# A conditioned convolution and feed-forward kernel: two more weight sums on GpSimd, one more convolution in short form, another order at both ends

## The chip, the cores and the metric

The kernel runs on one core of one Trainium2 chip. All data are fp32. The metric is the device time of one execution in microseconds (us). Engines are named as the profile names them: PE is TensorE's matmul, PEld its weight load, DVE is VectorE, ACT is ScalarE, POOL is GpSimd, SP is SyncE (used here to issue DMA transfers).

## The reference, cut to what matters

The input x has 128 samples of 64 channels by 1024 positions. Two layers are added to it, each a small mixing step followed by a matrix over the 1024 positions.

```python
def _L0_cond_ref(x, embedding, W0, b0, W1, b1, W2, b2, weight, bias_k):
    h = jax.nn.gelu(embedding @ W0 + b0, approximate=False)
    h = jax.nn.gelu(h @ W1 + b1, approximate=False)
    att = jax.nn.softmax((h @ W2 + b2) / T, axis=-1)
    agg_w = jnp.einsum('bk,koi->boi', att, weight[..., 0])   # 8 experts, 64x64, one matrix per sample
    agg_b = att @ bias_k
    return jnp.einsum('boi,bih->boh', agg_w, x) + agg_b[:, :, None]

def _L0_ffn_ref(x, A, B, bias):                              # rank 128
    return jnp.einsum('bsd,od->bso', x, A @ B.T) + bias

def _L1_cond_ref(x, c, weight, c_weight, bias):              # 9 taps, 4 groups of 16 channels
    out = lax.conv_general_dilated(x, weight, ..., padding=[(4, 4)], feature_group_count=4)
    return out + (c @ c_weight.T)[:, :, None] + bias[None, :, None]

def _L1_ffn_ref(x, W_up, gate_w, expert_bias, lora_A, lora_B):
    x_flat = x.reshape(-1, 1024)
    one_hot = top1(x_flat @ gate_w.T + expert_bias)          # 4 experts
    base_out = x @ W_up.T                                    # 1024 x 1024
    delta = lora_B[e] @ (lora_A[e] @ x_flat), e = one_hot    # rank 8
    return base_out + delta

x = x + _L0_ffn_ref(_L0_cond_ref(x, cond_128, ...), ...)
x = x + _L1_ffn_ref(_L1_cond_ref(x, cond_128, ..., fside_S_0), ...)
```

## The kernel before

**Tiles.** Two samples make a *pair* (`pr`, 64 of them), a tile of 128 partitions by 1024 columns that stays in SBUF from its load until its result is written to `out`. Two pairs make a *double-pair* (`d`, 32 of them), the unit of the second layer. Every engine's instructions run in the order in which the program writes them (`manual_schedule` over all five engines), so moving a line moves an instruction in its engine's queue.

**Layer 0, per pair.** `layer0_in` multiplies the turned tile `xt` (its own load, 512 KB) by B: 8 matmuls into a PSUM bank `pxb`, copied by ACT to `xb`. `layer0_mix` applies the sample's own 64x64 matrices: `pz`, and from it `z` (ACT for pairs 0 to 3, DVE after that). `layer0_out` multiplies by A: two halves `pd`, each added to x by DVE and written by SP to a DRAM tile `x1d`; two reads bring it back in another arrangement as `X`, the convolution's operand. With `later=True` these reads are issued where `back()` is called. The bias of layer 0's matrix is added to x in advance by `add_fbias` (POOL for most pairs).

**The convolution, per pair.** In the plain form 64 matmuls over `X` give both phases. In the short form, for pairs from `PLAIN` on, POOL makes two differences `df`, 16 matmuls with the summed weights `wsum` make a shared part `pm`, to which DVE adds the context; ACT copies it to the other partitions (`m2`), and only 32 matmuls over `df` remain (`pc`). `conv_out` (DVE) adds the shared part (or the context) and gives `yt`.

**W_up, per double-pair.** The 1024x1024 product is cut into blocks and multiplied in a form with fewer block products: `ffn_sums` makes 17 sums of blocks of `yt` (POOL), and `products` runs 26 block products of 4 matmuls each (`PRODUCTS`: the accumulator part `r`, the operand `u`, the W block `w`, and copies or additions that follow). The accumulators are the four PSUM banks `pb`, of two parts each. What is added straight to x (`"x"`) or from part to part (`"add"`, `"copy"`) goes to DVE and ACT. The W side of the form, 31 sums of W's blocks, is computed once, in place, in the opening: `W_SUMS` holds (target, first, sign, second), numbered from 0. Sums whose number is in `ON_POOL` go to POOL, others to DVE, where ACT first copies one operand into a PSUM bank `pw` unless it has just been computed or `aside` is false. The fifth entry of a row of `PRODUCTS` says how many W sums that product needs; `first_products` keeps the sums three products ahead. W comes in four loads of 1 MB, in the order 2, 1, 3, 0 of `load_w`.

**Gate and LoRA.** `gate_in` multiplies `yt` by the gate and LoRA-A weights (`pg`), `gate_out` copies it (ACT, `zg`), `gate` transposes it and chooses the expert on DVE, `turn` transposes the masked result (`pzt`, copied by ACT to `zt`), and `lora` adds it to the four banks with 4 matmuls. `results` drains the banks: DVE adds each to x, and SP writes both pairs to `out`, 512 KB each.

**Order.** The opening (before the loop over `d`) treats pairs 0 to 3 and makes the W sums between the products of double-pair 0. From `d = 1` the loop repeats: products 8 to 25 of `d`, then `tiles` (shared parts and convolutions of two later pairs, the gate of `d+1`, lora and results of `d`), then layer 0 of two further pairs around products 0 to 7 of `d+1`. In the last double-pair, `last_products` runs lora before product 20 and drains each bank when its last product is done (`LAST`: how many products, which bank).

**Queues that the change touches.** SP issues xt4, the four W loads, the `x1d` writes and `X` reads, x5's and later loads of the opening, and all of `out`. POOL runs `df`, the s sums, `add_fbias` of x4 and x5 and its own W sums in written order: in the kernel before, df2 and df3, then s sums 10 to 16, then the two ffn_bias additions, then W sums. Its issue queue loads later pairs (`load_x`).

Of the kernel before, what the change touches and what calls it, by code (L numbers as in the profile page):

```python
# [37 lines left out]
ALU = mybir.AluOpType  # L38
# [5 lines left out]
NPAIR = NB // 2  # L44
# [13 lines left out]
N = 512  # L58
NQ = N // 2
# [1 line left out]
NX = 3  # L61
NBD = 3
FIRST = 4
PLAIN = 2

# [41 lines left out]
    (2, 3, 12, 0, 31, ()),  # L109
)  # L110
NW = 26
ON_POOL = (16, 19, 20, 21, 23, 24, 27, 28)
LAST = ((21, 2), (24, 0), (25, 3), (26, 1))

PK = tuple(np.cumsum([0, P, P, 1, 1, P, 8, 8, CH, CH, E]).tolist())

# [2 lines left out]
def block(ctx: ExitStack, tc: tile.TileContext, a: dict, out: bass.AP):  # L119
    nc = tc.nc  # L120
# [32 lines left out]
    xs, xts, bds, aggbs, ctxs = {}, {}, {}, {}, {}  # L153

    def load_turned(pr, eng):
        xts[pr] = xtp.tile([P, NC, P], F32, tag="xt", name=f"xt{pr}")
        eng.dma_start(xts[pr], a["xt"][pr])
# [32 lines left out]
    def load_w(k, eng):  # L190

        eng.dma_start(W[:, 4 * k : 4 * k + 4].rearrange("p j c n -> p (j c n)"), a["wq"][k])

    def w_sums(upto, aside=True):

        for k in range(wdone[0], upto):
            to, x, op, y = W_SUMS[k]
            fresh = [W_SUMS[j][0] for j in range(max(k - 2, 0), k)]
            if op != "-" and x in fresh:
                x, y = y, x  # L200
            first = W[:, x]
            if k in ON_POOL:
                combine(nc.gpsimd, W[:, to], first, op, W[:, y])
                continue
            if aside and x not in fresh:
                first = bank(f"pw{k}")
                nc.scalar.copy(first, W[:, x].rearrange("p c n -> p (c n)"))
                first = first.rearrange("p (c n) -> p c n", c=QC)
            combine(nc.vector, W[:, to], first, op, W[:, y])
        wdone[0] = max(wdone[0], upto)  # L210
# [186 lines left out]
    def layer0_in(pr):  # L397
        xt = xts.pop(pr)
        pxb = bank(f"pxb{pr}")
        for c in range(NC):  # L400
            nc.tensor.matmul(pxb[:, :P], xt[:, c, :], bt[:, c, :], start=(c == 0), stop=(c == NC - 1))  # L401
        xb = xbp.tile([P, P], F32, tag="xb", name=f"xb{pr}")
        nc.scalar.copy(xb, pxb[:, :P])
        xbs[pr] = xb
# [17 lines left out]
    def layer0_out(pr, then=None, later=False):  # L422
        x, z0 = xs[pr], z0s.pop(pr)
        xt = X[pr % NX]
        d = x1d.tile([Q, P, P], F32, tag="x1d", name=f"x1d{pr}")
        dv = d.rearrange("q (c g) m -> (q c) g m", g=BG)
        h = P // 2
        for hf in range(2):
            cols = slice(hf * 512, (hf + 1) * 512)
            qs = slice(hf * Q // 2, (hf + 1) * Q // 2)  # L430
            pd = bank(f"pd{pr}_{hf}")
            nc.tensor.matmul(pd, z0, at[:, cols], start=True, stop=True)  # L432
            nc.vector.tensor_tensor(x[:, cols], pd, x[:, cols], ALU.add)  # L433
            nc.sync.dma_start(
                d[qs].rearrange("q r m -> r q m"), x[:, cols].rearrange("r (q m) -> r q m", m=P)
            )
        if then:
            then()

        def back():  # L440
            nc.sync.dma_start(xt[h:, :, :P], dv[:h])
            nc.sync.dma_start(xt[:h, :, 1 : P + 1], dv[h:])

        if later:
            return back
        back()
# [87 lines left out]
    def conv(pr):  # L534
        for b in range(2):
            conv_in(pr, b)
            conv_out(pr, b)
# [13 lines left out]
    def products(d, first, end):  # L551
        if not first:
            opened[d] = [psb.tile([P, N], F32, tag=f"pb{i}", name=f"pb{i}_{d}") for i in range(4)]
        for r, u, w, new, _, then in PRODUCTS[first:end]:
            p = part(d, r)
            if new == 2:
                nc.vector.memset(p, 0.0)
            for c in range(QC):
                nc.tensor.matmul(  # L559
                    p, ys[d][u][:, c], W[:, w, c], start=new == 1 and c == 0, stop=c == QC - 1, skip_group_check=True  # L560
                )
            for kind, to, op in then:
                if kind == "dcopy":
                    nc.vector.tensor_copy(part(d, to), p)
                elif kind == "copy" and op == "+":
                    nc.scalar.copy(part(d, to), p)
                elif kind == "copy":
                    nc.scalar.activation(part(d, to), p, AF.Copy, scale=-1.0)
                elif kind == "add":
                    copy = sums.tile([P, NQ], F32, tag="v", name=f"v{d}_{to}")  # L570
                    nc.scalar.copy(copy, p)  # L571
                    combine(nc.vector, part(d, to), part(d, to), op, copy)
                else:
                    x = xs[2 * d + to // 4][:, to % 4 * NQ : (to % 4 + 1) * NQ]
                    if op == "+":
                        nc.vector.tensor_tensor(x, p, x, ALU.add)  # L576
                    else:
                        nc.vector.scalar_tensor_tensor(x, p, -1.0, x, ALU.mult, ALU.add)  # L578

    def gate_in(d):  # L580

        yt = yts[d]
        pg = bank(f"pg{d}")
        for c in range(NC):
            for t in range(2):
                nc.tensor.matmul(  # L586
                    pg[t * GT : (t + 1) * GT, :P], gl[:, c, :], yt[:, t, c], start=c == 0, stop=c == NC - 1
                )
        return pg

    def gate_out(d, pg):
        zgs[d] = sp.tile([P, P], F32, tag="zg", name=f"zg{d}")
        nc.scalar.copy(zgs[d], pg[:, :P])
# [48 lines left out]
    def last_products(d, zm):  # L642

        zt = turn(d, zm)
        products(d, 17, LAST[0][0] - 1)
        lora(d, zt)
        at_ = LAST[0][0] - 1
        for end, b in LAST:
            products(d, at_, end)
            at_ = end  # L650
            x, cols = xs[2 * d + b // 2], (lo, hi)[b % 2]
            nc.vector.tensor_tensor(x[:, cols], opened[d][b], x[:, cols], ALU.add)
            nc.sync.dma_start(out[2 * d + b // 2][:, cols], x[:, cols])

    def add_fbias(pr, eng):
        eng.tensor_tensor(xs[pr], xs[pr], fbias, ALU.add)  # L656
# [68 lines left out]
    back1 = layer0_out(1, later=True)  # L725
    load_x(3, nc.sync)
    back1()
    load_turned(4, nc.sync)
    for k in (2, 1, 3, 0):
        load_w(k, nc.sync)  # L730
    wsum = const.tile([P, NGC, P], F32, tag="sel", name="wsum")
    nc.gpsimd.tensor_tensor(wsum, ws[:, :, 0], ws[:, :, 1], ALU.add)
    next(agg)
# [8 lines left out]
    add_fbias(3, nc.vector)  # L742
    w_sums(1, False)
    layer0_in(3)
    conv(1)
    w_sums(3)
    layer0_mix(3)
    back3 = layer0_out(3, later=True)
    back2()
    back3()  # L750
    agg_out()
# [1 line left out]
    load_cond(2)  # L753
    layer0_in(4)

    gate_out(0, gate_in(0))
    ffn_sums(0, 0, 10)
    done = [0]

    def first_products(n, most=len(W_SUMS)):  # L760
        for i in range(done[0], done[0] + n):
            w_sums(min(PRODUCTS[min(i + 3, len(PRODUCTS) - 1)][4], most))
            products(0, i, i + 1)
        done[0] += n
# [17 lines left out]
    w_sums(PRODUCTS[10][4])  # L782
    conv_out(3, 0)
    conv_out(3, 1)
    first_products(3)
    layer0_mix(4)
    first_products(1)
    layer0_out(4, lambda: load_x(6, nc.sync))
    layer0_in(5)
    first_products(1)  # L790
    layer0_mix(5)
    first_products(1)
# [4 lines left out]
    for d in range(NPAIR // 2):  # L797
        more = d + 1 < NPAIR // 2
        ahead = [pr for pr in (2 * d + 6, 2 * d + 7) if pr < NPAIR]
        if d and 2 * d + 5 < NPAIR:  # L800
            layer0_out(2 * d + 5)
        if 2 * d + 5 < NPAIR:
            load_context(d + 2)
        if ahead:
            load_cond(d + 3)
        if d:
            zm = gate(d)
        for pr, plus in zip((2 * d + 4, 2 * d + 5), (ahead, ())):
            if pr < NPAIR:
                differences(pr)  # L810
            for other in plus:
                add_fbias(other, nc.gpsimd)
        if not more:
            products(d, 8, 17)
            last_products(d, zm)
            break
        if d:
            products(d, 8, 23)
        else:
            first_products(2)  # L820
        zt = turn(d, zm)
        if d:
            products(d, 23, 26)
        else:
            first_products(2)
        tiles(d, zt, 2 * d + 4, 2 * d + 5)
        if more:
            ffn_sums(d + 1)
        for pr in (2 * d + 8, 2 * d + 9):
            if pr < NPAIR:  # L830
                load_x(pr)
        for pr in ahead:
            layer0_in(pr)
        if ahead:
            layer0_mix(ahead[0])
        if more:
            products(d + 1, 0, 4)
        if ahead:
            layer0_out(ahead[0])
            layer0_mix(ahead[1])  # L840
        if more:
            products(d + 1, 4, 8)
# [100 lines left out]
```

## Time and profile before

Three runs took 1276.84, 1277.93 and 1280.16 us (median 1277.93). One more was profiled.

| | |
|---|---|
| time of the profiled execution | 1276.48 us |
| its span, first to last instruction | 1274.7 us |
| mean granted TensorE clock | 0.999 of full speed |
| bytes moved by DMA | 189.72 MB, 149 GB/s on the mean |
| idle share by tenths of PE: slices 1 to 3 of 40 | busy 8, 8, 8 tenths |
| the other slices but the last | 9 tenths or more |
| the last slice | 8 tenths |
| costliest group: block products with sums, L559 | 2432 matmuls, 556.0 us, 379 ns each |

A slice is 31.9 us. On this page busy times are per engine, "x" counts instructions, "L559" is line 559 of the kernel before, and "out<-in" names the tiles with buffer numbers left out. In timelines the first number is the start in us from the span's start, the second the duration, and the bracket the idle time of that engine before the line and what ended it.

### The profile page before, as it was taken

The numbers are of one execution on the slowest core, as the hardware profiler recorded it, in microseconds if no ns is written. First come the engines' busy times: TensorE is split into PE (matmuls) and PEld (weight loads), VectorE is DVE, ScalarE is ACT, GpSimd is POOL, SyncE is SP. The second block draws the span as 40 slices with busy tenths as digits, with TensorE's granted clock in tenths as the row PEclk, the third lists the DMA queues.
The fourth block names the chain that finished last, engine by engine and source line by source line (L and its number), as shares of the span: only waits on it lengthen the run. The fifth ranks groups of instructions, "written<-read, shape, count | busy, mean of one in ns | idle before, by whom it ended". The sixth has DMA issues, their size and how long they took to land.

```text
span 1274.7 us, 23718 instructions
## 1 busy us (share of the span) xinstructions
PE 1256.7 (99%) x9255; PEld 1057.2 (83%) x9255; DVE 699.6 (55%) x1477; ACT 233.8 (18%) x586; POOL 730.3 (57%) x868
## 2 busy tenths in 40 slices
PE   8889999999999999999999999999999999999998
PEld 6668888888888888888888888888888888888886
DVE  6676555546545556555455555455555465455454
ACT  3231121111121111111211111111211111211111
POOL 1475676554676555676555676545775555765332
PEclk9999999999999999999999999999999999999999
DMA  9965544565444564444554444664434554445301
GB/s 311 343 159 161 149 140 113 143 176 162 140 130 114 159 176 157 138 121 114 176 176 149 142 113 125 176 174 151 135 104 141 176 174 134 130 118 148 104 34 67
DMA packets 184159, 189.72 MB, mean 149 GB/s; under 512 B 17392, under 2 KB 156656, under 8 KB 183536
## 3 DMA queue, kind: packets, MB, share of 16 engines
q1 hardware_dynamic: 166912, 126.07, 36.2%
q0 software_dynamic: 16128, 58.73, 13.6%
q10 hardware_dynamic: 1008, 3.41, 0.8%
q8 instruction: 74, 1.21, 0.4%
q14 instruction: 37, 0.30, 0.1%
HBM read 118.90 MB, written 69.27 MB: 148 GB/s over the span
## 4 chain that ended last, share of the span: by engine, by line
PE 93%; DMA 3%; DVE 2%; issue 0%; SPq 0%; ACT 0%; POOL 0%; DVEq 0%; ACTq 0%; POOLq 0%
PE pb L559 55%; PE pxb L401 9%; PE pd L432 8%; PE pc L515 8%; PE pm L477 4%; PE pg L586 4%; PE pb L631 3%; PE pz L411 1%; DMA w<-in_wq 1%; DMA x<-in_x 1%; DMA x1d<-x 1%; DVE yt L527 1%; DMA xt<-in_xt 0%; DVE w L216 0%; DMA X<-x1d 0%
## 5 line engine op out<-in xcount | busy, mean ns | idle before, releaser
L559 PE MATMUL pb<-w,s 128*128 128x256 f32 x2432 | 556.0, 379 | 4.9 <-DVE w L216 3.2
L559 PEld LDWEIGHTS pb<-w,s 128*128 128x128 f32 x2432 | 458.9, 190 | 70.5 <-DVE w L216 3.8
L469 POOL TENSOR_TENSOR df<-X 128x512 f32<-128x512 f32 x62 | 64.1, 1034 | 380.0 <-DMA X<-x1d 380.0
L559 PE MATMUL pb<-w,yt 128*128 128x256 f32 x896 | 225.6, 380 | 2.3 <-DVE x L637 1.7
L492 DVE TENSOR_TENSOR m<-pm,cx 64x512 f32<-64x512 f32 x124 | 85.4, 688 | 202.7 <-PE pm L477 199.8
L559 PEld LDWEIGHTS pb<-w,yt 128*128 128x128 f32 x896 | 162.8, 190 | 31.8 <-issue 8.7
L576 DVE TENSOR_TENSOR x<-pb,x 128x256 f32<-128x256 f32 x320 | 129.2, 421 | 94.0 <-PE pb L559 87.4
L216 POOL TENSOR_TENSOR s<-yt,s 128x256 f32<-128x256 f32 x224 | 165.3, 738 | 17.8 <-PE pb L559 2.8
L656 POOL TENSOR_TENSOR x<-x,ffn_bias 128x1024 f32<-128x1024 f32 x61 | 142.1, 2348 | 15.9 <-DMA x<-in_x 15.9
L401 PEld LDWEIGHTS pxb<-B,xt 128*128 128x128 f32 x1024 | 119.2, 194 | 25.2 <-DVE yt L527 22.0
L527 DVE TENSOR_TENSOR yt<-pc,m 128x512 f32<-128x512 f32 x124 | 122.8, 1110 | 22.4 <-ACT m L495 19.4
L432 PE MATMUL pd<-AT,z 128*128 128x512 f32 x256 | 122.8, 602 | 3.5 <-ACT z L417 2.8
L401 PE MATMUL pxb<-B,xt 128*128 128x128 f32 x1024 | 124.9, 280 | 0.0
L515 PE MATMUL pc<-ws,df 128*64 128x128 f32 x1984 | 113.6, 273 | 0.0
L433 DVE TENSOR_TENSOR x<-pd,x 128x512 f32<-128x512 f32 x128 | 88.3, 692 | 39.6 <-PE pd L432 32.2
L515 PEld LDWEIGHTS pc<-ws,df 128*64 128x64 f32 x1984 | 109.4, 137 | 0.0
L571 ACT COPY v<-pb 128x256 f32<-128x256 f32 x96 | 35.8, 373 | 372.0 <-PE pb L559 352.8
L216 POOL TENSOR_TENSOR s<-s,yt 128x256 f32<-128x256 f32 x128 | 93.9, 734 | 15.1 <-PE pzt L622 7.7
L495 ACT COPY m<-m 64x512 f32<-64x512 f32 x124 | 76.8, 619 | 133.6 <-DVE m L492 124.1
L216 POOL TENSOR_TENSOR s<-s,s 128x256 f32<-128x256 f32 x128 | 92.1, 730 | 5.0
L578 DVE SCALAR_TENSOR_TENSOR x<-pb,x 128x256 f32<-128x256 f32 x128 | 54.0, 422 | 67.8 <-PE pb L559 66.3
L637 DVE TENSOR_TENSOR x<-pb,x 128x512 f32<-128x512 f32 x124 | 76.6, 680 | 8.7 <-PE pb L631 8.7
(107 smaller groups left out, 918.2 us busy)
## 6 DMA issues: line engine op xcount, KB each, us to landing
x1d<-x SPq DMA_DIRECT2D x128, 256.0 KB, 4.4
X<-x1d SPq DMA_DIRECT2D x128, 256.0 KB, 4.4
out<-x SPq DMA_DIRECT2D x62, 512.0 KB, 3.6
xt<-in_xt POOLq DMA_DIRECT2D x56, 512.0 KB, 5.8
x<-in_x POOLq DMA_DIRECT2D x56, 512.0 KB, 6.2
cx<-ctxd SPq DMA_DIRECT2D x32, 128.0 KB, 4.3
w<-in_wq SPq DMA_DIRECT2D x4, 1024.0 KB, 12.2
ab<-aggbd SPq DMA_DIRECT2D x30, 128.0 KB, 3.4
```

The lines of the kernel that those rows point to most:

```text
L216: eng.tensor_tensor(to, x, y, ALU.add if op == "+" else ALU.subtract)
L401: nc.tensor.matmul(pxb[:, :P], xt[:, c, :], bt[:, c, :], start=(c == 0), stop=(c == NC - 1))
L432: nc.tensor.matmul(pd, z0, at[:, cols], start=True, stop=True)
L433: nc.vector.tensor_tensor(x[:, cols], pd, x[:, cols], ALU.add)
L492: nc.vector.tensor_tensor(by_group(m2[half, b]), by_group(pm[half]), context(pr, b, half), ALU.add)
L495: nc.scalar.copy(m2[other, b], m2[half, b])
L515: nc.tensor.matmul(pc[o * H : (o + 1) * H, cols], diffs[pr][:, 2 * g + b, o], ws[:, g, o], start=True, stop=True,)
L527: nc.vector.tensor_tensor(yt.rearrange("m q (o g two) -> m two g q o", two=2, g=NGC)[:, b], by_group(pcs.pop((pr, b))), context(pr, b) if ...
L559: nc.tensor.matmul(p, ys[d][u][:, c], W[:, w, c], start=new == 1 and c == 0, stop=c == QC - 1, skip_group_check=True)
L576: nc.vector.tensor_tensor(x, p, x, ALU.add)
L637: nc.vector.tensor_tensor(x[:, cols], b, x[:, cols], ALU.add)
L656: eng.tensor_tensor(xs[pr], xs[pr], fbias, ALU.add)
```

## The change

Six things are different.

1. `PLAIN` goes from 2 to 1: pair 1's convolution takes the short form, with its differences, shared part and `m2`, written out in the opening in place of `conv(1)`.
2. `ON_POOL` gets the W sums 11 (block 1 = block 5 − block 1) and 12 (block 5 = block 9 − block 10). On POOL, 11 comes behind s9, ahead of df2; 12 is the first of nine behind the two ffn_bias additions (eight stood there before). DVE's sum 13 (block 10 = block 6 + block 20) waits for 12, which reads block 10.
3. xt4's load is issued behind the first W load instead of ahead of all four.
4. Around pair 3 and the gate of double-pair 0, `w_sums(3)` comes after `layer0_mix(3)` and `layer0_out(3)` (z3 is then ahead of the copy pw2 on ACT, and the additions to x3 ahead of sums 1 and 2 on DVE); `w_sums(6)` comes between `gate_in(0)` and `gate_out(0)`.
5. `layer0_in(5)` comes right behind product 8, ahead of products 9, 10 and 11 and `layer0_out(4)`. Its PSUM bank is the one in which the first operand of sum 13 was copied.
6. Double-pair 30 also takes the path of `last_products`, and the gate of double-pair 31 follows it. `last_products` now runs lora behind product 20, and `LAST` also gives a column range: bank 1 is drained in two halves, one after product 21, one at the very end. Each double-pair of these two issues five writes to `out`.

```diff
-PLAIN = 2
+PLAIN = 1
...
-ON_POOL = (16, 19, 20, 21, 23, 24, 27, 28)
-LAST = ((21, 2), (24, 0), (25, 3), (26, 1))
+ON_POOL = (11, 12, 16, 19, 20, 21, 23, 24, 27, 28)
+
+LAST = ((21, 2, 0, N), (22, 1, NQ, N), (24, 0, 0, N), (25, 3, 0, N), (26, 1, 0, NQ))
...
         zt = turn(d, zm)
-        products(d, 17, LAST[0][0] - 1)
+        at_ = LAST[0][0]
+        products(d, 17, at_)
         lora(d, zt)
-        at_ = LAST[0][0] - 1
-        for end, b in LAST:
+        for end, b, f, t in LAST:
             products(d, at_, end)
             at_ = end
-            x, cols = xs[2 * d + b // 2], (lo, hi)[b % 2]
-            nc.vector.tensor_tensor(x[:, cols], opened[d][b], x[:, cols], ALU.add)
-            nc.sync.dma_start(out[2 * d + b // 2][:, cols], x[:, cols])
+            x = xs[2 * d + b // 2][:, b % 2 * N + f : b % 2 * N + t]
+            nc.vector.tensor_tensor(x, opened[d][b][:, f:t], x, ALU.add)
+            nc.sync.dma_start(out[2 * d + b // 2][:, b % 2 * N + f : b % 2 * N + t], x)
+        del xs[2 * d], xs[2 * d + 1], opened[d]
...
     back1()
-    load_turned(4, nc.sync)
     for k in (2, 1, 3, 0):
         load_w(k, nc.sync)
+        if k == 2:
+            load_turned(4, nc.sync)
...
     layer0_in(3)
-    conv(1)
-    w_sums(3)
+    differences(1)
+    shared_in(1)
+    conv_in(1, 0)
+    shared_out(1)
+    conv_in(1, 1)
+    conv_out(1, 0)
+    conv_out(1, 1)
     layer0_mix(3)
     back3 = layer0_out(3, later=True)
+    w_sums(3)
     back2()
...
-    gate_out(0, gate_in(0))
+    pg = gate_in(0)
+    w_sums(6)
+    gate_out(0, pg)
...
-    first_products(3)
+    first_products(1)
+    layer0_in(5)
+    first_products(2)
     layer0_mix(4)
     first_products(1)
     layer0_out(4, lambda: load_x(6, nc.sync))
-    layer0_in(5)
     first_products(1)
...
-        if not more:
+        if 2 * d + 4 >= NPAIR:
             products(d, 8, 17)
             last_products(d, zm)
-            break
+            if more:
+                gate_out(d + 1, gate_in(d + 1))
+                ffn_sums(d + 1)
+                products(d + 1, 0, 8)
+            continue
```

## The prediction

> **What bounds the kernel now.** I read the busy shares first, then the chain of waits, then PE's timeline at both ends.
>
> ```profile
> span 1274.7 us, 23718 instructions
> PE 1256.7 (99%) x9255; PEld 1057.2 (83%) x9255; DVE 699.6 (55%) x1477; ACT 233.8 (18%) x586; POOL 730.3 (57%) x868
> ...
> 92.80:131.30 38.50, 38.50 (x287) 32.63 (x286) 20.85 (x44) 6.75 (x17) 24.19 (x29) 1.00 0.52 150
> ```
>
> PE is the bound. The third line is the windows view of one steady iteration (PE, weight loads, DVE, ACT, POOL, then clock, DMA share, GB/s): PE is busy for all of its 38.50 us. Nothing in the diff changes that loop from d=1 to d=29, so the change can act only in the opening (before about 93 us, where pm4 starts the loop) and in the last two double-pairs. The opening acts by one number: how much later or earlier the loop starts. The tail acts by PE's waits after 1219 us and by what follows PE's last matmul.
>
> PE's timeline, lines with the idle time in brackets (start, duration):
>
> ```profile
> 43.82 3.63 PE L432 MATMUL pd<-AT,z 128*128 128x512 f32 x4 [2.42 <-ACT z L417]
> ...
> 65.75 1.13 PE L559 MATMUL pb<-w,yt 128*128 128x256 f32 x4
> 69.83 1.99 PE L559 MATMUL pb<-w,s 128*128 128x256 f32 x8 [2.94 <-DVE w L216]
> 71.66 0.38 PE L411 MATMUL pz<-bd,xb 128*128 128x128 f32 x2
> ...
> 73.54 1.98 PE L432 MATMUL pd<-AT,z 128*128 128x512 f32 x4
> 75.36 1.95 PE L401 MATMUL pxb<-B,xt 128*128 128x128 f32 x16
> ```
>
> The first wait is for z3, which ACT computes behind the copy for W sum 2. The 4 matmuls after it took 3.63 against 1.98 us: the clock fell. At 65.75 stands product 8, at 69.83 products 9 and 10, which waited for DVE's W sums 12 to 14, at 73.54 pd4, at 75.36 pxb5.
>
> **The opening: what goes.** z3 is now computed ahead of that copy: at most 2.42 + (3.63 − 1.98) = 4.1 us of PE time are freed. Pair 1's short form has 16 + 32 matmuls in place of 64; by the rows of the same kind (pm x32 in 1.80, so 16 in 0.90; short pc x64 from 62.16 to 65.75, so 32 in 1.80) it is 2.70 against 3.65 us, −0.95. Its additions lie beside other work: two df on POOL (1.04 each) while POOL idles up to 42 us; the two m additions and two copies of pair 1 on DVE and ACT, of the 1.4 and 1.4 us that half of the x4 rows show. So PE would come to product 8 at about 62 instead of 65.75.
>
> **The opening: what comes.** That lead meets POOL's queue.
>
> ```profile
> 57.36 1.04 POOL L469 TENSOR_TENSOR df<-X 128x512 f32<-128x512 f32 x1 [0.17 <-DMA X<-x1d]
> 58.35 1.04 POOL L470 TENSOR_TENSOR df<-X 128x512 f32<-128x512 f32 x1
> 59.35 3.03 POOL L216 TENSOR_TENSOR s<-s,s 128x256 f32<-128x256 f32 x4
> ...
> 64.55 4.68 POOL L656 TENSOR_TENSOR x<-x,ffn_bias 128x1024 f32<-128x1024 f32 x2
> 69.18 8.11 POOL L216 TENSOR_TENSOR w<-w 128x512 f32<-128x512 f32 x6
> 78.91 2.50 POOL L216 TENSOR_TENSOR w<-w 128x512 f32<-128x512 f32 x2 [1.61 <-DVE w L216]
> ```
>
> W sum 12 becomes a POOL instruction, and by its place in the program it stands behind both ffn_bias additions (L656). POOL works in order. Its chain starts with X3, which landed at 57.2. That time should stay: in the windows from 40.50 to 47.30 the DMA share is 1.02 and 1.03, so the queue is full and bytes, not z3, set it (xt4's load changes place among W's blocks, not in amount). Then df3 to 59.4, seven s sums to 64.55, the ffn_bias pair to 69.2 (x5 itself lands at 65.35), W sum 12 at 1.25 (half of the 2.50 row) to 70.45. DVE's sum 13 overwrites block 10, which sum 12 reads, so it waits: 0.69 more, 71.15.
>
> pxb5 now stands right behind product 8, and needs the PSUM bank that sum 13 reads. So PE stops at 62 and goes on at 71.25: a wait of about 9 us in place of 2.42 and 2.94. Behind pxb5 wait products 9 to 11, pz4 and pd4, and on SP behind pd4's results everything from the x1d4 write on.
>
> Warm, from 71.25: pxb5 1.79 (75.36 to 77.15), which covers DVE's sum 14 (1.95 in its row at 67.83, beside a busy POOL, 0.69 in its shortest rows; product 9 needs it), products 9 and 10 1.73 (the x8 row from 81.29 to the next at 83.02), so pz4 is at 74.8; from pz4 to pd4 it was 1.88 (71.66 to 73.54), of which DVE's sum 15 held some 0.5; I take 1.4, so pd4 is at 76.2. With an untouched clock that is 2.7 late.
>
> What a 9 us wait does to the clock no row shows. Bounds: nothing, since after the 2.94 us wait the clock stayed 1.00; and twice the 1.65 us which the 2.42 us wait cost.
>
> ```profile
> 43.80:47.30 3.50, 3.48 (x5) 1.42 (x6) 1.67 (x3) 0.00 (x0) 3.27 (x5) 0.53 1.03 378
> 66.90:69.83 2.93, 0.00 (x1) 0.00 (x1) 2.76 (x4) 0.69 (x2) 2.93 (x3) 1.00 0.05 9
> ```
>
> I take 1.65, once: the wait is longer than both, so a drop is more likely than none, and the one drop seen was a single stretch of some 3.4 us. Then pd4 is at 77.85, +4.3; bounds +2.7 and +6.0.
>
> [...]
>
> **From pd4 to the loop.** pxb5 (1.8) no longer follows pd4, so PE alone would be late by 4.3 − 1.8 = 2.5. But pd4 also starts the transfers: x1d4 out, xt6 and x6 in, X4 back, x1d5, xt7, x7, X5. From 77 to 94 us the DMA share is 1.07, so their train can't be squeezed, and it arrived just in time:
>
> ```profile
> 93.72 1.04 POOL L469 TENSOR_TENSOR df<-X 128x512 f32<-128x512 f32 x1 [0.72 <-DMA X<-x1d]
> ```
>
> POOL waited for X5, which landed at 93.56; pm5, half-way in the x32 row of 92.79, started at 93.77. So the slack was 0.2, and the loop starts 4.3 − 0.2 = +4.1 later.
>
> **W sum 11** also goes to POOL, behind s9 (before: 49.49 to 50.2), where POOL then waited 4.93 us for X2: 1.25 us cost nothing. Without that cover it would push df2 and with it all of POOL's chain by 1.25. pw11 and pw12 leave ACT, which is busy 18%: nothing. The copies for sums 3 to 5 now run ahead of zg0, which is first used at 86.47 by pgt0, and x3's additions ahead of sums 1 and 2, whose products come after 51 us: nothing either.
>
> **The tail.**
>
> ```profile
> 1246.22 1.13 PE L559 MATMUL pb<-w,yt 128*128 128x256 f32 x4 [0.78 <-DVE x L637]
> ...
> 1264.43 1.14 PE L631 MATMUL pb<-lb,zt 32*128 32x512 f32 x8 [0.45 <-ACT pb L566]
> ```
>
> Double-pair 30 now drains bank by bank, and pg31 (1.9 us, row 1242.41) covers the last drain: −0.78. lora behind product 20 gives ACT's copy time: −0.45. The last DVE addition is half as wide, 0.42 (256 columns) against 0.69: −0.27. The last transfer is 128 KB instead of 256; 256 KB took 2.03 from issue to landing and 512 KB 2.64, so halving is worth some 0.2 (0 to 0.3). Sum −1.7, bounds −1.2 and −2.1: at the low end ACT's copy or the drain of bank 2 still holds PE for part. In d=30 five output issues instead of two lie on an SP that has nothing else there, and zg31's copy comes later but still 5 us ahead of pgt31. The 0.97 us wait at 1219.54 stays.
>
> **Sum.** +4.1 − 1.7 = +2.4. The profiled execution took 1276.48 us (span 1274.7 and 1.8 around it), so it would be 1278.9; it is 1.45 under the median of the three runs, 1277.93, on which scale the forecast is 1280.3.
>
> **Rivals.**
>
> *The transfers do not bind* (pm5 is late only by PE's own 2.5): +0.8, 1278.7. [...] Against: the 1.07 share and the 0.72 wait.
>
> *Slower: the clock falls for two stretches in the long wait.* Place: pxb5 to pd4, behind the wait for sum 13. Price 3.3 instead of 1.65, so 76.2 + 3.3 − 73.54 − 0.2 = +5.8 − 1.7 = +4.1, 1282.0. It decides from a loss of 3.1 us. For it: the wait is 3.5 times the one that caused a drop. Against: the drop on record lasted 3.4 us, and pxb5 with two products is as long as that.
>
> *Faster: the sums on POOL are not in the way*, and the change does what a shorter opening should: PE keeps its 3.9 us, −3.9 − 1.7 = −5.6, 1272.3. For it: z3's wait does go, and X3 could land earlier with it. Against: the ffn_bias pair (4.68 us) stands in POOL's queue ahead of sum 12, and x5's landing at 65.35 alone puts sum 12 at 65.35 + 2.34 + 1.25 = 68.9 at the earliest, 69.6 with DVE's sum, which leaves at best 1.6 us less than my 71.15.
>
> **How the numbers follow.** Chances: forecast 0.47, transfers not binding 0.16, slower 0.26, faster 0.11. What a measurement of this kernel can tell from no change is about 0.3%, 3.8 us. Forecast and first rival lie within it, so faster 0.11, same 0.62 (0.63 less a little for the forecast's upper bound), slower 0.27. Range: the low end is the first rival with no clock loss and the full tail, 2.5 − 1.65 − 2.1 = −1.25, 1276.7; the high end the slow rival with the short tail, 5.8 − 1.2 = +4.6, 1282.5; three runs before spread by 3.3 us, so each end is given 0.7 to 1: 1276 to 1283.5. The faster case stays out.
>
> **What would show it.** Right: a PE wait of 8 to 9 us before pxb5 at about 71, released by DVE's or POOL's w; pd4 at 76 to 79.5; the x3 row around 43 without its 2.42 and at 1.98; POOL's ffn_bias pair still ending at 69.2; X5 landing at 97 to 98; pm4 3 to 4 us later than 92.79; no wait at 1246 and 1264 (shifted). Wrong: pxb5 before 68, X3 landing before 56, or a loop of another length than 38.5 us.

## The result, and the profile after

Thirteen runs of the changed kernel took 1278.91 to 1283.44 us, median 1281.06; thirteen of the kernel before 1275.12 to 1280.16, median 1278.34. The ratio is 1.0026, with a 95% interval of 1.0017 to 1.0034: slower by some 3 us of 1278 (2.7 between the medians), which is inside the 0.3% bound and close to the forecast of 1280.3. The profiled execution took 1282.76 us (span 1281.0), 1.7 above its median, while the one before lay 1.9 below its own; so the two traces differ by 6.3 us of span, and not all of that belongs to the change. Their mean granted clocks are 0.995 and 0.999.

PE's timeline after the change (start, duration, in brackets idle time before and who ended it; lines of code were added above, so L401 is now L402, and L656 is L658):

```profile
37.74 1.10 PE L478 MATMUL pm<-wsum,X 128*64 128x128 f32 x16 [0.89 <-DMA X<-x1d]
...
39.83 1.96 PE L516 MATMUL pc<-ws,df 128*64 128x128 f32 x30 [0.56 <-POOL df L471]
41.73 0.49 PE L412 MATMUL pz<-bdx,xb 128*128 128x128 f32 x2
...
43.04 1.98 PE L433 MATMUL pd<-AT,z 128*128 128x512 f32 x4 [0.42 <-ACT z L418]
...
62.55 1.13 PE L560 MATMUL pb<-w,yt 128*128 128x256 f32 x4
71.85 3.78 PE L402 MATMUL pxb<-B,xt 128*128 128x128 f32 x16 [8.16 <-DVE w L217]
75.42 2.77 PE L560 MATMUL pb<-w,s 128*128 128x256 f32 x8
...
79.30 1.98 PE L433 MATMUL pd<-AT,z 128*128 128x512 f32 x4
...
99.72 1.10 PE L478 MATMUL pm<-wsum,X 128*64 128x128 f32 x16 [2.05 <-DMA X<-x1d]
100.62 3.24 PE L587 MATMUL pg<-yt,gl 128*64 128x128 f32 x32
103.58 4.14 PE L516 MATMUL pc<-ws,df 128*64 128x128 f32 x64
107.65 1.14 PE L632 MATMUL pb<-lb,zt 32*128 32x512 f32 x8
```

The wait for z3 is gone (0.42 us is left, pd3 at 1.98), product 8 comes at 62.55 instead of 65.75, and then PE stands for 8.16 us. pd4 is at 79.30 instead of 73.54. Later pm5 waits another 2.05 us for X5, and the gate and convolution behind it run slow (3.24 against 1.95 us, 4.14 against 3.69). The same rows in the kernel before, up to the first lora:

```profile
92.79 2.00 PE L477 MATMUL pm<-wsum,X 128*64 128x128 f32 x32
94.59 1.95 PE L586 MATMUL pg<-yt,gl 128*64 128x128 f32 x32
96.34 3.69 PE L515 MATMUL pc<-ws,df 128*64 128x128 f32 x64
99.96 1.14 PE L631 MATMUL pb<-lb,zt 32*128 32x512 f32 x8
```

The chain of waits of the changed kernel between 55 and 105 us (start, duration, what) tells why:

```profile
58.05 1.04 POOL df L470
59.09 1.00 POOL df L471
60.09 0.69 POOL s L217
...
63.16 2.09 POOL s L217 x3
65.24 1.67 POOL x L658
...
67.51 2.34 POOL x L658
69.85 1.23 POOL w L217
71.10 0.70 DVE w L217
71.85 3.78 PE pxb L402 x16
75.63 2.56 PE pb L560 x8
...
79.30 2.00 PE pd L433 x4
...
82.03 2.73 DMA x1d<-x
...
85.50 6.87 DMA x1d<-x
...
93.06 6.53 DMA X<-x1d
99.72 1.10 PE pm L478 x16
```

POOL works through df3, the s sums, the ffn_bias additions (x L658) and then W sum 12; DVE's sum 13 follows at 71.10 and releases PE. Behind pd4 the chain goes through DVE's addition to x4 and then through transfers until pm5.

The windows view, cut at the changes of the granted clock (the first figure behind the five busy times with their counts):

```profile
63.50:66.95 3.45, 0.18 (x1) 0.00 (x0) 2.02 (x2) 1.00 (x2) 3.45 (x4) 1.00 0.47 176
66.95:71.85 4.90, 0.00 (x1) 0.01 (x1) 0.72 (x2) 0.18 (x1) 4.90 (x4) 0.50 0.10 29
71.85:77.19 5.34, 5.34 (x21) 4.98 (x22) 3.81 (x5) 0.85 (x2) 5.26 (x5) 0.50 0.01 3
77.19:101.08 23.89, 21.25 (x120) 16.05 (x120) 13.71 (x33) 5.73 (x13) 12.40 (x10) 1.00 0.78 190
101.08:104.49 3.41, 3.41 (x37) 3.41 (x35) 1.58 (x3) 2.25 (x5) 3.17 (x5) 0.50 0.00 0
123.46:161.96 38.50, 38.50 (x287) 32.61 (x287) 20.79 (x45) 6.73 (x17) 22.98 (x27) 1.00 0.54 156
```

The clock was at half (0.50) from 66.95 to 77.19 and from 101.08 to 104.49. PE worked 5.34 + 3.41 us of that, and half of it, an estimated 2.67 + 1.71 us, is lost time. The last row is the loop, unchanged.

The tail of the changed kernel, PE and DVE:

```profile
1245.80 1.14 PE L632 MATMUL pb<-lb,zt 32*128 32x512 f32 x8
...
1251.38 1.97 PE L587 MATMUL pg<-yt,gl 128*64 128x128 f32 x32
1253.28 1.13 PE L560 MATMUL pb<-w,yt 128*128 128x256 f32 x4
...
1271.83 1.14 PE L632 MATMUL pb<-lb,zt 32*128 32x512 f32 x8
```

```profile
1277.52 0.42 DVE L653 TENSOR_TENSOR x<-pb,x 128x256 f32<-128x256 f32 x1 [0.17 <-PE pb L560]
```

No brackets at either lora nor between the gate and the first product: the waits of 0.45 and 0.78 us are gone.

### The profile page after: what moved, and what is told of

Its sections match the earlier page's. It is cut to its first block, busy times and chain, and to the rows that moved or that the text cites. A ratio compares the mean times of both kernels' runs of the same rounds, so it can differ in the third digit from the quotient of the medians.

```text
span 1281.0 us, 23698 instructions
## 1 busy us (share of the span) xinstructions
PE 1258.7 (98%) x9239; PEld 1060.1 (83%) x9239; DVE 698.9 (55%) x1479; ACT 233.5 (18%) x586; POOL 734.9 (57%) x872
## 3 DMA queue, kind: packets, MB, share of 16 engines
q10 hardware_dynamic: 1008, 3.41, 0.7%
## 4 chain that ended last, share of the span: by engine, by line
PE 92%; DMA 5%; POOL 1%; DVE 1%; issue 0%; SPq 0%; ACT 0%; POOLq 0%; DVEq 0%
PE pb L560 55%; PE pxb L402 9%; PE pc L516 8%; PE pd L433 8%; PE pm L478 4%; PE pg L587 4%; PE pb L632 3%; DMA x1d<-x 3%; DMA X<-x1d 2%; PE pz L412 1%; DMA ffn_bias<-in_ffn_bias 1%; POOL s L217 0%; POOL x L658 0%; PE pgt L599 0%; PE pzt L623 0%
## 5 line engine op out<-in xcount | busy, mean ns | idle before, releaser
L658 POOL TENSOR_TENSOR x<-x,ffn_bias 128x1024 f32<-128x1024 f32 x61 | 142.2, 2348 | 16.6 <-DMA x<-in_x 16.6
L402 PEld LDWEIGHTS pxb<-B,xt 128*128 128x128 f32 x1024 | 120.5, 196 | 32.7 <-DVE yt L528 22.0
L402 PE MATMUL pxb<-B,xt 128*128 128x128 f32 x1024 | 126.6, 283 | 8.2 <-DVE w L217 8.2
L516 PE MATMUL pc<-ws,df 128*64 128x128 f32 x2016 | 116.4, 273 | 0.6 <-POOL df L471 0.6
L433 PEld LDWEIGHTS pd<-AT,z 128*128 128x128 f32 x256 | 48.0, 190 | 37.4 <-issue 29.4
```

Of the source, the lines that this page charges most:

```text
L516: nc.tensor.matmul(pc[o * H : (o + 1) * H, cols], diffs[pr][:, 2 * g + b, o], ws[:, g, o], start=True, stop=True,)
```

## The experiments

Each kernel was timed against the kernel before on the same chip (the experiments took three chips in all); the ratio is that of the two, with its 95% interval, and kernels of different rows are compared by it. From each trace I read four numbers: the start of product 8, of pd4, of the first lora (where the loop has begun), and the span.

| kernel | product 8 | pd4 | lora | lora − pd4 | span | span − lora | ratio to before |
|---|---|---|---|---|---|---|---|
| before | 65.75 | 73.54 | 99.96 | 26.42 | 1274.7 | 1174.7 | |
| changed | 62.55 | 79.30 | 107.65 | 28.35 | 1281.0 | 1173.4 | 1.0026 [1.0017, 1.0034] |
| sum12_early | 61.57 | 70.94 | 97.05 | 26.11 | 1270.4 | 1173.4 | 0.9978 [0.9966, 0.9990] |
| sums_on_dve | 62.51 | 75.18 | 101.15 | 25.97 | 1274.6 | 1173.5 | 0.9986 [0.9974, 0.9997] |
| tail_only | 67.98 | 74.93 | 101.82 | 26.89 | 1275.2 | 1173.4 | 0.9996 [0.9984, 1.0009] |
| filled_wait | 61.63 | 83.35 | 109.63 | 26.28 | 1283.0 | 1173.4 | 1.0073 [1.0056, 1.0091] |
| filled_half | 61.21 | 75.45 | 101.27 | 25.82 | 1274.6 | 1173.3 | 1.0013 [1.0002, 1.0024] |
| pxb5_back | 62.53 | 77.78 | 104.18 | 26.40 | 1277.5 | 1173.3 | 1.0026 [1.0017, 1.0035] |
| x7_late | 63.91 | 80.92 | 107.23 | 26.31 | 1280.6 | 1173.4 | 1.0035 [1.0023, 1.0048] |
| early_x7 | 62.34 | 70.18 | 96.16 | 25.98 | 1269.5 | 1173.3 | 0.9968 [0.9956, 0.9979] |
| s12_plain | 62.97 | 72.29 | 98.04 | 25.75 | 1271.3 | 1173.3 | 0.9977 [0.9964, 0.9990] |
| s12_xt4 | 63.49 | 73.63 | 99.55 | 25.92 | 1272.9 | 1173.4 | 0.9974 [0.9963, 0.9986] |
| p910_first | 61.77 | 68.42 | 93.26 | 24.84 | 1266.7 | 1173.4 | 0.9939 [0.9924, 0.9954] |
| pxb5_last | 62.80 | 70.73 | 97.87 | 27.14 | 1271.3 | 1173.4 | 0.9962 [0.9950, 0.9973] |

Behind the first lora all kernels with the new tail agree within 0.2 us. What differs between kernels, and between executions of one kernel, lies in the first 110 us.

**sum12_early: W sum 12 ahead of df2 on POOL.**

```diff
     first_products(8, PRODUCTS[8][4])
+    w_sums(13)
     differences(2)
```

> The changed kernel with W sum 12 moved in POOL's order from behind the two ffn_bias additions to right behind W sum 11, ahead of df2 and df3; nothing else differs. Theory (POOL's order delays sum 12, and it holds pxb5): sum 12 ends near 56 instead of 71, sum 13 then follows yt2 on DVE and ends near 67.2, pxb5 starts at 67 to 68 instead of 71.85, PE waits 3.5 to 4.5 us there instead of 8.16, pd4 stands at 72.5 to 74.5 instead of 79.30, and the time is 1 to 2.5 us below the kernel before (0.998 to 0.9995 of it), some 4 to 5 us below the changed one. Rival (the short form of pair 1, xt4's place or pxb5's place cause the loss): pxb5 may start earlier, but the time stays 2 to 3 us above the kernel before (1.002).

Median 1273.86 against 1276.85 us, 0.9978. In its trace PE waits 2.19 us where it waited 8.16, at full clock (1.00 from 60 to 100 us):

```profile
64.89 2.05 PE L402 MATMUL pxb<-B,xt 128*128 128x128 f32 x16 [2.19 <-DVE w L217]
...
70.94 1.98 PE L433 MATMUL pd<-AT,z 128*128 128x512 f32 x4
```

POOL's two sums now stand in one row ahead of df2, in a gap:

```profile
51.20 2.63 POOL L217 TENSOR_TENSOR w<-w 128x512 f32<-128x512 f32 x2 [0.50 <-ACT pw L208]
55.03 1.04 POOL L470 TENSOR_TENSOR df<-X 128x512 f32<-128x512 f32 x1 [1.21 <-DMA X<-x1d]
```

By these ratios one line of order turns the change from 0.26% slower into 0.22% faster. The cause of the loss is shown: not that POOL does sum 12, but where it stands in POOL's queue. pd4 was earlier than expected (72.5 to 74.5), because pxb5 was: DVE's sum 13 follows yt2, and yt2 started at 62.28 instead of 64.48, as in the changed kernel.

```profile
62.28 2.03 DVE L528 TENSOR_TENSOR yt<-pc,m 128x512 f32<-128x512 f32 x2 [2.30 <-DMA aggd<-agg]
```

This row also shows the next limit, which the prediction did not see. yt2 takes the buffer from which half of the samples' own matrices (agg, 1 MB) is being written to DRAM, and DVE waits for the end of that write: 2.30 us here and 3.34 in the changed kernel. In the kernel before, yt2 started at 64.38 without a wait. So much of the 2.19 us that PE still waits is likely this.

**sums_on_dve: both sums back on DVE**, all else as changed (`ON_POOL` as before).

> The changed kernel with W sums 11 and 12 back on DVE (ON_POOL as before); all other parts of the change stay. Theory: DVE does sums 12 and 13 behind yt2, at 66.5 to 68, so pxb5 starts near 68 and pd4 near 73 to 75; the time is level with the kernel before up to 2 us below it (0.9985 to 1.000). Rival (the loss lies in the other parts): it stays 2 to 3 us above the kernel before (1.002), with pd4 at 77 or later.

0.9986, pd4 at 75.18, just past the late end of what the theory had. The wait at pxb5 was 3.68 us and the clock fell (3.78 us for pxb5, against 2.05 in sum12_early). So without the two sums on POOL the change no longer loses, and is likely worth a small gain (the interval ends at 0.9997); sum 12 in its place took that and more.

**tail_only: the kernel before with the change of the last two double-pairs.**

> The kernel before with only the change of the last two double-pairs (LAST, last_products, the path of double-pair 30). Theory: the waits of 0.78 and 0.45 us and a third of the last drain go; span 1.4 to 1.7 us shorter, ratio 0.9987 to 0.999. Rival (the last transfer or the output queue ends the span anyway): no change, ratio 1.000, with the last output's landing at the same distance behind PE's last matmul as before.

The ratio can't tell 1.4 us from none (its interval holds 0.999 and 1.000). The trace can: from the first lora to the end it took 1173.4 us instead of 1174.7, the same 1.3 to 1.4 as in all other kernels with this tail. Its opening, which is that of the kernel before, came to pd4 1.4 us later than in the other profile of the same opening; this is the scatter that hides the gain.

**filled_wait and filled_half: PE kept busy in the wait**, 37 or 19 matmuls of a zero tile that add nothing.

```diff
     first_products(1)
+    for _ in range(37):
+        nc.tensor.matmul(part(0, 6), zeros, at[:, :NQ], start=False, stop=True, skip_group_check=True)
     layer0_in(5)
```

> The changed kernel with 37 matmuls of a zero tile, 256 columns each (0.216 us each when warm, 8 us in all), between product 8 and pxb5; they add zero to an accumulator, and all else is as in the changed kernel. Theory (the long wait costs a clock drop on top): PE has no wait of 8 us, the clock stays 1.00 at pxb5, pxb5 starts near 71 to 72 and takes 1.95 instead of 3.78, pd4 stands at 76 to 77 instead of 79.30, and the time is 2 to 3 us below the changed kernel, so level with the kernel before (0.999 to 1.001). Rival (pd4 waits for z4 or for a landing, not for PE's clock): pd4 stays at 79 and the time stays 2 to 3 us above the kernel before.

> As filled_wait, but with 19 of the zero matmuls: the trace of filled_wait shows each as two of 0.218 us, so 37 took 16.14 us and held pxb5 until 78.57; 19 take 8.3, the length of the wait. Theory: pxb5 starts at 71.5 to 72.5 at full clock, pd4 4.8 us after it (as in filled_wait: 78.57 to 83.35) and not 7.45 as in the changed kernel, so at 76.3 to 77.3; the time is 2 to 3 us below the changed kernel, 0.999 to 1.001 of the kernel before. Rival (the clock's loss is hidden, because the transfers to X5 bind from another start than pd4): the time stays 2 to 3 us above the kernel before (1.002).

The first had the wrong size: each matmul stands twice in the trace, 37 took 16.14 us, and pxb5 was held until 78.57 (1.0073). Even so it shows the clock's part, since from pxb5 to pd4 it took 4.78 us instead of 7.45. The second had the right size:

```profile
62.18 8.36 PE L800 MATMUL pb<-AT,zeros 128*128 128x256 f32 x38
70.56 2.05 PE L404 MATMUL pxb<-B,xt 128*128 128x128 f32 x16
...
75.45 1.98 PE L435 MATMUL pd<-AT,z 128*128 128x512 f32 x4
```

4.89 us from pxb5 to pd4 and clock 1.00 from 60 to 100 us, so in the profiled execution the fallen clock cost 2.6 us (7.45 − 4.89). Ten of the twelve runs had a mean granted clock of 1.000 and the other two 0.998, while none of the changed kernel's thirteen was above 0.997. The ratio is 1.0013: by medians 1.0 us above the kernel before instead of 2.7. That puts the clock at some 1.7 us of the median and the wait itself at the rest, but loosely, because the intervals of the two ratios overlap; 1.0013 is also just above the range expected.

**pxb5_back: layer0_in(5) behind layer0_out(4) again.**

> The changed kernel with layer0_in(5) back behind layer0_out(4), as before the change; the two sums stay on POOL. Theory (the transfers behind pd4 bind, so a step ahead of pd4 costs and one behind it is free): product 9 waits for sum 14 until 73, pd4 stands 1 to 2.5 us earlier than 79.30, pm5 still waits for X5, and the time is 1 to 2.5 us below the changed kernel (1.0005 to 1.002 of the kernel before). Rival (PE's own work binds and the place of pxb5 in the wait helps): pd4 earlier, but products 11 to 25 later by pxb5, no wait of pm5 for X5, and the time level with the changed kernel or up to 1 us above it.

pd4 was 1.5 us earlier (77.78), pm5 did not wait for X5, and the time was level with the changed kernel (1.0026 both). pm5 and the time went as the rival had it, but the intervals, some 1.1 us to either side, do not exclude the low end of the theory's gain, and in the two profiled executions lora stands 3.5 us earlier here, 1.7 of it the second clock drop that this one did not have. From pd4 to lora PE's own work takes 26.40 us without pxb5 ahead of pd4; with it, and with xt7 and x7 in their old place, the kernels whose clock did not fall behind pd4 take 25.8 to 26.3, bound by the transfers. The two limits lie within some 0.6 us, so what the place of pxb5 earns as the transfers stand is too small for these times to show.

**x7_late: xt7 and x7 loaded behind X5's reads.**

```diff
-    layer0_out(5, lambda: load_x(7, nc.sync))
+    layer0_out(5)
+    load_x(7, nc.sync)
```

> The changed kernel with the loads of xt7 and x7 (1 MB) behind the two reads of X5 in SP's order instead of ahead of them. Theory (bytes ahead of X5 set its landing): X5 lands 2 to 3 us earlier after pd4 than in the changed kernel, pm5's wait of 2.05 us goes, the clock stays 1.00 in pg1 and pc4 (another 1.7 us), and the time is 2 to 3.5 us below the changed kernel, unless x7's later landing holds POOL's addition to x7 and df5 behind it. Rival (the train is set by the round trip's own latency): X5 lands at the same distance behind pd4 and the time stays.

X5 came early enough (pm5 started without a wait, 18.2 us behind pd4 instead of 20.4), but POOL then waited for x7:

```profile
100.93 2.36 POOL L658 TENSOR_TENSOR x<-x,ffn_bias 128x1024 f32<-128x1024 f32 x1 [3.83 <-DMA x<-in_x]
103.25 1.04 POOL L470 TENSOR_TENSOR df<-X 128x512 f32<-128x512 f32 x1
```

and held df5 behind it, so that PE waited 0.34 and 0.57 us in pc5: the exception that the expectation names. 1.0035: no gain. It is the changed kernel's fault again, an ffn_bias addition ahead of what PE needs.

**early_x7, p910_first, pxb5_last: towards a better version.** early_x7 is sum12_early with DVE's sums 13 and 14 ahead of yt2 (both operands from SBUF), x7_late's order, and x7's ffn_bias addition behind df5. p910_first also puts products 9 and 10 ahead of pxb5 and loads xt7 and x7 behind the context of the loop's first iteration; pxb5_last is the same with layer0_in(5) behind pd4. The core of p910_first against the changed kernel:

```diff
     first_products(8, PRODUCTS[8][4])
+    w_sums(13)
...
     shared_out(3)
+    w_sums(PRODUCTS[10][4], False)
     conv_in(3, 0)
...
-    w_sums(PRODUCTS[10][4])
...
-    first_products(1)
-    layer0_in(5)
-    first_products(2)
+    first_products(3)
+    layer0_in(5)
     layer0_mix(4)
...
-    layer0_out(5, lambda: load_x(7, nc.sync))
+    layer0_out(5)
...
+        if not d:
+            load_x(7, nc.sync)
...
-        for pr, plus in zip((2 * d + 4, 2 * d + 5), (ahead, ())):
+        for pr, plus in zip((2 * d + 4, 2 * d + 5), (ahead, ()) if d else (ahead[:1], ahead[1:])):
```

> A version meant to be the best of both: the changed kernel with W sum 12 right behind sum 11 on POOL, DVE's sums 13 and 14 ahead of yt2 (without the copy of an operand into PSUM), xt7 and x7 loaded behind X5's reads, and the ffn_bias addition to x7 behind df5. Theory: PE's wait at pxb5 shrinks from 8.16 us to 1 to 2, pd4 stands at 67.5 to 69.5 instead of 79.30 (73.54 before, 70.94 in sum12_early), pm5 waits for X5 under 1 us; the time is 2 to 4 us below sum12_early, so 5 to 7 us below the kernel before (0.9945 to 0.996). Rival (something else holds the loop's start, such as x6 or bd or ACT's copies): no more than 1 us below sum12_early (0.997 to 0.998).

> early_x7 with two more moves: products 9 and 10 ahead of pxb5 (their W sums are ready, while pxb5 waits 1.82 us for the bank that yt2 drains), and xt7 and x7 loaded behind the context and matrices of the loop's first iteration, whose late context held DVE's m4 and PE by 0.59 and 0.35 us. Theory: pd4 stands 5.5 to 6.5 us after product 8 instead of 7.84, no wait in pc4 and pc5, and the time is 1 to 2.5 us below early_x7 (0.9945 to 0.996 of the kernel before). Rival (pd4 then waits for bd, z4 or x4's ffn_bias addition): as early_x7.

> As p910_first, but with layer0_in(5) behind pd4, as in the kernel before. Theory (pd4 starts the transfers, and the loop starts 26.1 us after it): pd4 earlier than in p910_first by up to 1.8 us, as far as bd, z4 and x4 let it, and the loop's start earlier by at most that; PE itself then binds. The time is level with p910_first or up to 1 us below. Rival (X5 doesn't bind any more, PE's work does): level with p910_first within 0.3 us, with pm5 free of a wait in both.

early_x7 gained, but less than expected (0.9968; pd4 at 70.18; 25.98 us from pd4 to lora, since m4 on DVE waited for its context, now queued behind xt7 and x7). p910_first beats both kernels, by slightly more than expected: median 1268.77 against 1277.27 us, 0.9939 [0.9924, 0.9954]. All five runs had a mean clock of 1.000, and they lie within 1.4 us. Its opening on PE has hardly a gap left:

```profile
62.74 1.92 PE L560 MATMUL pb<-w,s 128*128 128x256 f32 x8
64.75 2.05 PE L402 MATMUL pxb<-B,xt 128*128 128x128 f32 x16
...
68.42 1.98 PE L433 MATMUL pd<-AT,z 128*128 128x512 f32 x4
...
86.99 1.10 PE L478 MATMUL pm<-wsum,X 128*64 128x128 f32 x16 [0.20 <-DMA X<-x1d]
```

Here pxb5 ahead of pd4 does pay: lora stands 24.84 us behind pd4, which is PE's 26.42 of before less 1.79 for pxb5, plus 0.2 of waiting for X5. pxb5_last (0.9962) failed its expectation the other way: without pxb5 as cover, pz4 waited 1.70 us for bd and product 11 waited 1.11 us for DVE's sum 15, the clock fell once more (0.88 on the mean from 62 to 76 us, against 1.00 in p910_first), and pd4 stood later, not earlier.

**s12_plain and s12_xt4: one small part of the change undone, on top of sum12_early** (pair 1 in the plain form; xt4's load ahead of W's).

> sum12_early with pair 1's convolution in the plain form again (PLAIN 2, conv(1) in its place); only this part of the change is undone. The prediction's step: the short form saves PE 0.95 us, so from pxb3's end to pz3 it takes longer here than the 3.99 us of sum12_early (36.40 to 40.39), and the time is 0.5 to 1 us above sum12_early. Rival, from the traces of the runs so far (PE waits 0.56 us for df1 between pm1 and pc1, and 3.99 us is more than the 3.65 of the kernel before, 36.85 to 40.50): here it takes 3.65, unless X1 is late, and the time is level with sum12_early or 0.3 us below.

> sum12_early with xt4's load ahead of all four W loads, as in the kernel before; only this part is undone. Theory: the bytes are the same, so X3 lands within 0.5 us of sum12_early's and the time is level with it (0.997 to 0.9985 of the kernel before). Rival (the first W load landing earlier matters, as it feeds sum 0 and sums 1 and 2): W's sums 0 to 2 and product 0 are 1 us later, and so are product 8 and the time, by up to 1 us.

s12_plain: 0.9977 against 0.9978, level. From the start of the convolution to pz3 it took 3.65 us (38.47 to 42.12) against 3.99 in the short form, so in the traces the short form of pair 1 saves PE nothing: it has fewer matmuls, but PE waits for df1. The times alone, with intervals of 1.5 us to either side, could not tell. s12_xt4: 0.9974, level too. In its profile z3 was late again by 0.9 us (a wait of 1.36 instead of 0.42) and product 8 by 1.9, of which 0.9 stood already at pxb3 (35.43 against 34.53), ahead of the first W block's use; in the time none of it shows. Part 4 of the change (z3 and the W sums) was not run by itself; what it is worth is read from the traces alone.

## Why the prediction was right, and which of its steps were not

- **POOL's queue: right, nearly to the tenth.** Forecast: df3 until 59.4, ffn_bias until 69.2, sum 12 until 70.45, sum 13 until 71.15, pxb5 at 71.25. Measured: 60.1, 69.85, 71.08, 71.80, 71.85; the whole chain was 0.6 to 0.7 later because POOL got X2 0.7 later (df2 at 55.88 instead of 55.15) and df3 followed df2 without a wait. sum12_early shows that this order made the loss: with it alone changed, the kernel is faster than the one before.
- **Product 8 at 62: right (62.55), but not by its sum.** The two gains named, 4.1 and 0.95, would give 60.7. Measured up to pxb4 (44.87 instead of 47.24): 2.00 of the wait for z3 and 1.65 of the clock were gained, 0.34 was lost in the convolution and 0.89 in a new wait for X1; a further 0.8 came behind it, mostly because a wait of 1.68 became 1.16. "−0.95" for the short form of pair 1 was wrong in sign: 3.99 us against 3.65. The step put df1 beside other work, "while POOL idles up to 42 us"; but PE's own pc1 needs it, two differences of 1.04 us one after the other before the odd half can go on. POOL's idle time did not hide work that PE waited for (0.56 us ahead of 39.83).
- **The clock: mis-sized.** I took 1.65 us with bounds 0 and 3.3. The long wait cost 2.67 in the profiled execution, and some 1.7 of the median by filled_half. A second drop, 1.71 us behind pm5's wait of 2.05, was in no step. At the place that the slower rival names, pxb5 to pd4, the loss is nearer its 3.3 than my 1.65, though short of the 3.1 from which it decides; with the second drop the profiled execution lost 4.4 and took 1282.76, while the median stayed below the rival's 1282.0.
- **pd4 late by 4.3: 5.8 in the trace.** Of the 1.5 more, 0.6 is X2's and 1.0 the clock's.
- **W sum 11 at nothing: right.** It ran from 52.53 to 53.80 on POOL, which then still waited 2.07 us for X2.
- **The transfers behind pd4 bind: right in kind.** pm5 waited for X5 in every kernel that had pxb5 ahead of pd4 and xt7 and x7 in their old place, 1.1 to 2.05 us; moving xt7 and x7 let PE go at 24.84. The 20 us from pd4 to X5 on which the sum rests held (20.0 before, 20.3 after; X5 landed at 99.6 and not at 97 to 98, because pd4 was later). But "the loop starts 4.3 − 0.2" set the consequence of the wait at nothing: pm5 was 6 us later than before, and lora, behind the second drop, 7.7.
- **The tail: −1.7 forecast, −1.3 to −1.4 measured.** The two waits (0.78, 0.45) and a third of the last drain (0.27), 1.5 together, went nearly as worked out. The term "−0.2" for the smaller last transfer was wrong: a write of 128 KB took 2.0 us from issue to landing, like one of 256 KB, and from the last DVE instruction's end to the end of the span it is 3.06 us (before 3.02).
- **The net**: +2.4 forecast, +2.7 between the medians. By the traces alone it would be +6.3. The step that put both on the scale of one profiled execution hid that the opening of the kernel before also scatters: the same opening stood 1.4 us later at pd4 in tail_only than in the profile from which the sum was made. That profile was of a good execution: its mean clock was 0.999, while the kernel before had 0.997 to 0.998 on the mean over the 80 runs beside the experiments. Most of these runs thus had a lower clock than the traced one, and the changed kernel lost more to the clock than the sum gave it; left out on both sides, the two offset in part. Part of the good agreement is therefore luck: too small a loss was weighed against too early a start.

## What to carry to other kernels

Work moved to an idle engine goes to the place in its queue where the program writes it, and it is that queue's contents, not the engine's idle share, that price it (here PE waited 8.16 us with W sum 12 behind the ffn_bias additions and 2.19 with it ahead of df2): look for what stands ahead of it and who waits behind it. A move that fails by its place may gain when it is moved once more, as here by one line (1.0026 to 0.9978). Where several limits lie within a microsecond or two (PE's work, the transfers, one engine's order), removing one alone may show nothing, as in pxb5_back and x7_late (1.0026 and 1.0035), and here the version that moves several of them together gained most (p910_first, 0.9939).

## What the runs showed that was not expected

In these traces the length of a wait did not decide alone whether the granted clock fell. In the kernel before it fell behind the 2.42 us wait (0.50 from 44.01 to 47.42) and not behind the longer one of 2.94 (1.00 from 66.90 to 75.40); in the changed kernel it fell in the wait of 8.16, and again behind the 2.05 us ahead of 99.72. Other traces agree: the matmuls behind 2.12 us in tail_only took 3.68 us against 1.98, and pxb5 behind 2.49 us in s12_xt4 took 3.50, while it took 2.05 behind 2.19 us in sum12_early and behind 2.28 in s12_plain. Nor did the clock come back as soon as PE worked again: in the changed kernel it rose at 77.19 and at 104.49, 5.34 and 4.77 us after PE had gone on, in the kernel before 3.60 us after. The stretches at half clock lasted 10.24 and 3.41 us in the changed kernel, with 23.89 us between them, and 3.41 us in the kernel before. What decides besides the length was not shown.

In most of the kernels the scatter between executions goes with this clock. By the mean granted clock of each of the changed kernel's runs, the one at 0.997 took 1278.91 us, the six at 0.996 had a median of 1280.2, the five at 0.995 one of 1282.35, and the one at 0.993 took 1283.44. The kernel before shows the same on each of the three chips: its runs at 0.999 or more have medians 1.8 to 3.5 us below those at 0.996 or less. p910_first, which has hardly a wait left, had 1.000 in every run. Why the clock falls more often in some runs was not shown, since one execution of each kernel was profiled; and some scatter has another source (one run of filled_half took 1280.55 us at 1.000, and the ten runs of pxb5_back, all at 0.995 or 0.996, show no such order).
